# Values of the selected tokens by their own product in the last batch, and a new order of steps for the last two batches

## The chip, the core and the metric

The kernel runs on one core of a Trainium2 chip. The metric is the time of one execution on the device in microseconds (us), the median of several. The core has five engines that run side by side, each with its own queue of instructions in a fixed order: TensorE (PE in the profile: matmuls and transposes), VectorE (DVE), ScalarE (ACT), GpSimd (POOL) and SyncE (SP). SP, ACT and POOL also issue DMAs.

## What is computed

Two layers on x of 8 batches x 512 channels x 32 x 32 tokens, all in float32. Layer 0 is a group norm, attention with 8 heads over 1024 tokens and a residual. Layer 1, which the change is about, selects 256 of the 1024 tokens of each batch by the sum of their squares, lets these attend to each other, and puts the result in place of their values:

```
q, kk, v = wq x, wk x, wv x                      # over the channels
importance = sum(x * x over the channels);  idx = top 256
q_sel, k_sel = layer_norm(q[idx]), layer_norm(k[idx])
attn = softmax(clip(q_sel k_sel^T * 512**-0.5, -80, 80))
v[idx] = attn v[idx]
out = x + wo v
```

## The kernel before

Layer 0 takes most of the time; its values, x1, go to DRAM. Before layer 1 the matrices wv and wo are multiplied into one (`w["vo"]`), so that V of a token holds its contribution to the output, and the last product of the reference falls away: attended values are written over the rows of V, and V is only transposed and added to x1.

Layer 1 is written as small steps, each a function of a batch b and a number i (L235 to L547). For one batch they are, in order of the data:

- row (four transposes of x1 to rows of tokens), square (sum of squares on ScalarE), keep (copy of the rows to one of four buffers xT), put (a DMA from there to DRAM, sx)
- finite, spread, imp: the importances as a column and as a row; count (eight of them, VectorE): how many tokens are ahead of each; place, pick, holder, who: the indices of the selected tokens
- getx: GpSimd gathers the selected rows from sx. vo (four matmuls of 512 columns, in float32 eight records each), vkeep (copy to V in SBUF), vput (to DRAM, sv): V of 128 tokens; eight of these for a batch. getv gathers V of the selected tokens from sv to the tile vs
- selt, selk: the selected rows transposed to selT; qk (four products); stats, root, norm: layer norm; normt, scale: transposed and scaled; score, clip, exp, inv, probt, probk: softmax; att (two products with vs), attk, attput: result to DRAM, sa
- fetch (eight): GpSimd gathers from sa into V those rows that belong to selected tokens; back (eight): transposes of V; add (eight): plus x1, whose piece y was loaded by residual, and the store to the output. SP issues y's loads and the stores

The order on TensorE, VectorE, ScalarE and GpSimd is written out by hand as lists of words. BATCH holds one turn of the loop over the batches; a sign behind a word says how many batches ahead (+) or behind (-) the step works, so the work of several batches is interleaved. END is the list behind the last turn; in it a word without sign is of batch 7, one minus is batch 6, two are batch 5, and so on. Each engine executes its own steps of the list in that order and waits where data or a buffer isn't ready. SP's order isn't fixed by the list. All products and transposes of layer 1 write into PSUM tiles of one kind, of which there are eight in turn (bank, L221), so each waits for the readers of the tile eight before it. y has six buffers, and four loads are issued ahead (L520, L570).

Of the kernel before, what the change touches and what calls it, by code (L numbers as in the profile page):

```python
# [55 lines left out]

BATCH = """
# [13 lines left out]
vput7-- put2- keep1- add3---- square1- att0--- put1- holder-- inv--- who-- row0- vkeep6--  # L71
back4---- square2- row6- attk0--- row3- back7---- add7---- att1--- square0- back6----
add4---- row7- keep0- put4- square6- row5- keep6- keep7- attk1--- vo1- vo0- vput0-- put0-
getx-- square3- square5- add6---- keep3- attput--- square7- fetch1--- keep5- finite- selt1--
spread0- spread1- vkeep1- imp1- vput5-- imp0- put6- selt0-- fetch6--- count5- fetch5---
selk0-- fetch3--- selk1-- vo3- qk0-- count7- vkeep0- count6- count3- qk1-- fetch0--- put5-
qk2-- stats1-- stats0-- root1-- fetch2--- vkeep3- back0--- root0-- vo4- qk3-- stats2--
count2- fetch4--- root2-- norm0-- vput0- norm1-- vkeep4- put3- add0--- stats3-- root3--
normt0-- vo2- vput2-- norm2-- vput4-- vput6-- normt1-- row4 scale1-- norm3-- normt2--
normt3-- vput1-- vkeep2- scale2-- scale0-- square4 keep4 fetch7--- scale3-- count1- vo5-  # L80
count0- score1-- back5--- score0-- put7- add5--- clip-- vput3-- vo6- count4- place- vo7-
vkeep5- exp-- pick0- vkeep7- back3--- row1 probt-- vkeep6- back1--- inv-- add1--- probk--
row2 keep1 square2 square1 back2--- getv-- put1 back4--- att0-- add3--- add2--- vput1- keep2
row7 pick1- row0 row3 row6 put4 holder- keep0 square7 square3 back7--- put2 keep7 attk0--
add4--- who- add7--- att1-- row5 getx- square5 vo0 keep3 square0 attk1-- attput-- fetch5--
fetch4-- square6 put0 vput5- vo1 back6--- fetch1-- finite keep6 selt1- selt0- keep5 spread0
vkeep0 spread1 imp0 imp1 selk0- add6--- selk1- vo3 vput7- vput3- count2 vkeep1 fetch2--
# [29 lines left out]
def attention_then_topk_attention(  # L117
# [231 lines left out]
    def gather(name, pool, src):  # L349
        def step(b, _):  # L350
            t = get(pool, (name, b), [P, RT, C], name, 2)
            for rb in range(RT):
# [5 lines left out]
                    bounds_check=N - 1, oob_is_err=False,  # L358
                )
        return step  # L360


    def selt(b, j):
        pt = bank(("st", b, j)).rearrange("p (a n) -> p a n", n=TOP)
# [186 lines left out]
    def layer1():  # L551
        with ExitStack() as st:
# [16 lines left out]
            with tc.manual_schedule(engines=ORDERED):  # L569
                for _ in range(4):  # L570
                    residual(*next(loads))
# [646 lines left out]
```

## Time and profile before

| | us |
|---|---|
| median of 3 runs (2642.01 to 2644.24) | 2642.17 |
| the profiled execution | 2641.74 |
| its span, first to last instruction | 2640.0 |
| TensorE busy in it | 2578.1 (98%) |
| VectorE busy | 1922.1 (73%) |
| ScalarE busy | 1352.7 (51%) |
| GpSimd busy | 1163.8 (44%) |
| END, about | 2452 to 2640 |

Layer 1 begins at about 2120, layer 0 fills what is before. The profile's page cuts the span into 40 slices and gives each engine's busy share in tenths; the table of stretches has the busy us of PE, its weight loads, DVE, ACT and POOL in turn, then the granted clock of TensorE, the share of the DMA engines and GB/s. In lists of waits and in the timeline, "<-" names what ended an engine's idle time. In a timeline's line the numbers are the start, the time taken, the engine, the line of the kernel, the operation and its tiles, written to the left of "<-" and read to the right.

### The profile page before, as it was taken

The numbers are of one execution on the slowest core, as the hardware profiler recorded it, in microseconds if no ns is written. First come the engines' busy times: TensorE is split into PE (matmuls) and PEld (weight loads), VectorE is DVE, ScalarE is ACT, GpSimd is POOL, SyncE is SP. The second block draws the span as 40 slices with busy tenths as digits, with TensorE's granted clock in tenths as the row PEclk, the third lists the DMA queues.
The fourth block names the chain that finished last, engine by engine and source line by source line (L and its number), as shares of the span: only waits on it lengthen the run. The fifth ranks groups of instructions, "written<-read, shape, count | busy, mean of one in ns | idle before, by whom it ended". The sixth has DMA issues, their size and how long they took to land.

```text
span 2640.0 us, 27385 instructions
## 1 busy us (share of the span) xinstructions
PE 2578.1 (98%) x9916; PEld 1185.7 (45%) x9916; DVE 1922.1 (73%) x2434; ACT 1352.7 (51%) x1698; POOL 1163.8 (44%) x559
## 2 busy tenths in 40 slices
PE   7999999999999999999999999999999999999995
PEld 4444444444444444444444444444443345555553
DVE  5688868886878678867877787777767556666664
ACT  3556655565566456644665465556555433333331
POOL 0456645555455455544564465446545511211122
PEclk9999999999999999999999999999999999999998
DMA  3000001000100010011000100010002243555556
GB/s 132 1 5 32 1 24 56 17 1 31 58 9 1 32 64 1 1 32 64 0 1 32 64 1 7 27 64 1 13 28 88 76 168 124 199 203 203 196 187 199
DMA packets 79590, 161.21 MB, mean 61 GB/s; under 512 B 12106, under 2 KB 12106, under 8 KB 79456
## 3 DMA queue, kind: packets, MB, share of 16 engines
q1 hardware_dynamic: 52480, 113.27, 12.3%
q10 hardware_dynamic: 19296, 33.58, 3.4%
q0 software_dynamic: 7680, 12.61, 1.6%
q8 instruction: 79, 1.29, 0.2%
q14 instruction: 55, 0.45, 0.1%
HBM read 100.68 MB, written 71.30 MB: 65 GB/s over the span
## 4 chain that ended last, share of the span: by engine, by line
PE 90%; DMA 3%; DVE 3%; ACT 1%; issue 1%; POOL 1%; ACTq 0%; SPq 0%; POOLq 0%; DVEq 0%
PE sc L930 18%; PE av L989 17%; PE g L727 16%; PE g L748 8%; PE g L766 8%; PE b_pv L299 5%; PE b_pp L382 4%; PE ns L967 2%; PE den L1002 2%; PE pt L953 2%; DMA sx<-xT 1%; PE b_sc L448 1%; PE first L727 1%; PE b_po L527 1%; DMA y<-x1d 1%
## 5 line engine op out<-in xcount | busy, mean ns | idle before, releaser
L981 POOL TENSOR_TENSOR es<-es,e 128x1024 f32<-128x1024 f32 x384 | 913.6, 2379 | 345.2 <-ACT e L976 324.4
L938 ACT COPY e<-sc 128x1024 f32<-128x1024 f32 x512 | 508.1, 1013 | 568.4 <-PE sc L930 308.6
L973 DVE TENSOR_TENSOR e<-e,ns 128x1024 f32<-128x1024 f32 x512 | 603.9, 1206 | 2.5 <-PE ns L967 2.2
L976 ACT ACTIVATE e<-e 128x1024 f32<-128x1024 f32 x512 | 531.4, 1056 | 114.5 <-DVE e L973 107.8
L944 DVE TENSOR_TENSOR high<-sc,high 128x1024 f32<-128x1024 f32 x384 | 469.6, 1223 | 122.8 <-PE sc L930 56.8
L930 PE MATMUL sc<-q,k 64*128 64x512 f32 x2048 | 509.6, 615 | 4.8 <-DVE high L944 1.8
L989 PE MATMUL av<-e,v 128*64 128x512 f32 x2048 | 492.7, 602 | 0.0
L981 POOL TENSOR_TENSOR es<-e,e 128x1024 f32<-128x1024 f32 x64 | 151.4, 2366 | 706.6 <-ACT e L976 706.6
L727 PE MATMUL g<-x,wqkv 128*128 128x512 f32 x992 | 453.0, 599 | 0.0
L930 PEld LDWEIGHTS sc<-q,k 64*128 64x128 f32 x2048 | 176.0, 186 | 328.9 <-issue 180.6
L727 PEld LDWEIGHTS g<-x,wqkv 128*128 128x128 f32 x992 | 178.5, 190 | 228.0 <-issue 224.2
L989 PEld LDWEIGHTS av<-e,v 128*64 128x64 f32 x2048 | 129.9, 136 | 300.8 <-issue 293.7
L1014 DVE RECIPROCAL ri<-ri 128x512 f32<-128x512 f32 x64 | 214.6, 3353 | 26.2 <-ACT ri L1010 25.8
L748 PE MATMUL g<-wqkv,x 128*128 128x256 f32 x992 | 230.5, 385 | 0.0
L766 PE MATMUL g<-o,wp 128*128 128x512 f32 x472 | 219.9, 609 | 2.7 <-ACT V L313 2.7
L748 PEld LDWEIGHTS g<-wqkv,x 128*128 128x128 f32 x992 | 183.4, 190 | 68.0 <-issue 44.7
L299 PE MATMUL b_pv<-w,x 128*128 128x512 f32 x448 | 199.0, 592 | 0.0
L958 DVE TENSOR_REDUCE nm<-pt 128x8 f32<-128x1024 f32 x64 | 78.4, 1225 | 146.7 <-PE pt L953 146.4
L773 DVE SCALAR_TENSOR_TENSOR xr<-g,pb,xr 128x512 f32<-128x512 f32 x56 | 42.0, 749 | 170.8 <-PE g L766 170.8
L766 PEld LDWEIGHTS g<-o,wp 128*128 128x128 f32 x472 | 85.4, 191 | 134.1 <-issue 112.7
L1010 ACT COPY ri<-den 128x512 f32<-128x512 f32 x64 | 37.5, 585 | 178.6 <-PE den L1002 135.1
L299 PEld LDWEIGHTS b_pv<-w,x 128*128 128x128 f32 x448 | 82.5, 190 | 90.5 <-issue 90.2
(165 smaller groups left out, 1980.1 us busy)
## 6 DMA issues: line engine op xcount, KB each, us to landing
x<-in_x_dram SPq DMA_DIRECT2D x32, 512.0 KB
x<-x1d SPq DMA_DIRECT2D x32, 512.0 KB
sv<-V ACTq DMA_DIRECT2D x64, 256.0 KB
sx<-xT ACTq DMA_DIRECT2D x64, 256.0 KB
y<-x1d SPq DMA_DIRECT2D x64, 256.0 KB
out_dram<-y SPq DMA_DIRECT2D x64, 256.0 KB
xr<-in_x_dram SPq DMA_DIRECT2D x58, 256.0 KB
x1d<-xr SPq DMA_DIRECT2D x58, 256.0 KB
```

The costliest lines, as they stand in the source:

```text
L299: nc.tensor.matmul(pv, x1[b][:, k, ts(j, P)], w["vo"][:, k, :], start=(k == 0), stop=(k == CT - 1),)
L727: nc.tensor.matmul(pq, wqkv[:, k, ts(ot, P)], hs[b][:, k, ts(hf, HALF)], start=(k == 0), stop=(k == CT - 1),)
L748: nc.tensor.matmul(pv[:, ts(j, 2 * P)], hs[b][:, k, ts(2 * part + j, P)], wqkv[:, k, 2 * C + hm * 2 * P : 2 * C + (hm + 1) * 2 * P], start ...
L766: nc.tensor.matmul(po, wp[:, k, ts(mt, P)], os[b * NPAIR + k][:, ts(hf, HALF)], start=(k == 0), stop=(k == CT - 1),)
L930: nc.tensor.matmul(sc[:, hh, :], ks[p][r, ts(j, P)], qs[p][r, ts(hf, HALF)], start=True, stop=True,)
L938: nc.scalar.copy(raw[t, j], banks["s", t, j])
L944: nc.vector.tensor_tensor(high[t], banks["s", t, j], raw[t, 0] if j == 1 else high[t], ALU.max)
L973: nc.vector.tensor_tensor(raw[t, j], raw[t, j], high[t], ALU.add)
L976: nc.scalar.activation(raw[t, j], raw[t, j], AF.Exp, scale=QK_SCALE)
L981: nc.gpsimd.tensor_add(sums[t], raw[t, 0] if j == 1 else sums[t], raw[t, j])
L989: nc.tensor.matmul(avs[t][HD * hh : HD * hh + HD, :], vs[p // 2][:, j, (p % 2) * P + HD * hh : (p % 2) * P + HD * hh + HD], e[:, hh, :], s ...
L1014: nc.vector.reciprocal(dens[t], dens[t])
```

## The change

A new step vsel multiplies selT (the selected rows of x1, transposed, which qk uses anyway) by `w["vo"]`: four matmuls for each of two blocks of 128 selected tokens. vselk copies the result to the tile vs. In batch 7 alone these two take the place of getv, and the eight vput of batch 7 are left out, since nothing reads them. The vo steps of batch 7 stand among and behind the steps of its attention. The list END is new as a whole, also for batches 3 to 6; the other steps in it are the same ones, each as often as before. y gets eight buffers instead of six, and six loads are issued ahead instead of four.

```diff
--- before.py
+++ after.py
@@ -68,37 +69,36 @@
 getv- add2-- pick1 row2+ probt- vkeep7 row1+ probk- keep2+
 """
 END = """
-vput7-- put2- keep1- add3---- square1- att0--- put1- holder-- inv--- who-- row0- vkeep6--
-back4---- square2- row6- attk0--- row3- back7---- add7---- att1--- square0- back6----
-add4---- row7- keep0- put4- square6- row5- keep6- keep7- attk1--- vo1- vo0- vput0-- put0-
-getx-- square3- square5- add6---- keep3- attput--- square7- fetch1--- keep5- finite- selt1--
-spread0- spread1- vkeep1- imp1- vput5-- imp0- put6- selt0-- fetch6--- count5- fetch5---
-selk0-- fetch3--- selk1-- vo3- qk0-- count7- vkeep0- count6- count3- qk1-- fetch0--- put5-
-qk2-- stats1-- stats0-- root1-- fetch2--- vkeep3- back0--- root0-- vo4- qk3-- stats2--
-count2- fetch4--- root2-- norm0-- vput0- norm1-- vkeep4- put3- add0--- stats3-- root3--
-normt0-- vo2- vput2-- norm2-- vput4-- vput6-- normt1-- row4 scale1-- norm3-- normt2--
-normt3-- vput1-- vkeep2- scale2-- scale0-- square4 keep4 fetch7--- scale3-- count1- vo5-
-count0- score1-- back5--- score0-- put7- add5--- clip-- vput3-- vo6- count4- place- vo7-
-vkeep5- exp-- pick0- vkeep7- back3--- row1 probt-- vkeep6- back1--- inv-- add1--- probk--
-row2 keep1 square2 square1 back2--- getv-- put1 back4--- att0-- add3--- add2--- vput1- keep2
-row7 pick1- row0 row3 row6 put4 holder- keep0 square7 square3 back7--- put2 keep7 attk0--
-add4--- who- add7--- att1-- row5 getx- square5 vo0 keep3 square0 attk1-- attput-- fetch5--
-fetch4-- square6 put0 vput5- vo1 back6--- fetch1-- finite keep6 selt1- selt0- keep5 spread0
-vkeep0 spread1 imp0 imp1 selk0- add6--- selk1- vo3 vput7- vput3- count2 vkeep1 fetch2--
-count5 fetch0-- fetch3-- fetch7-- put5 count3 qk0- stats0- qk1- root0- count7 qk2- stats1-
-norm0- count6 root1- qk3- put3 vkeep3 stats2- stats3- vo2 vo4 put6 root2- root3- back0--
-norm3- norm2- norm1- fetch6-- vkeep2 count0 add0-- normt2- back5-- vput4- vput6- vkeep4
-normt1- normt3- scale2- vput4 normt0- add5-- scale3- scale1- vo5 scale0- score1- put7 vput2-
-count1 count4 place back1-- pick1 score0- back2-- vo6 vkeep5 clip- add2-- pick0 vo7 holder
-exp- probt- add1-- vput0 vkeep6 getv- vkeep7 probk- back3-- back4-- who back6-- att1- att0-
-inv- back7-- attk0- attk1- vput2 getx add3-- selt0 add4-- attput- selk0 add7-- fetch0-
-fetch7- selt1 selk1 vput6 fetch3- qk0 stats0 add6-- qk2 fetch1- qk1 root0 fetch2- stats2
-root2 norm2 stats1 root1 qk3 fetch6- norm0 back0- stats3 vput7 norm1 normt1 root3 vput3 norm3
-fetch4- vput1 normt2 fetch5- scale2 vput5 back1- normt3 scale3 normt0 scale1 scale0 add0-
-add1- getv score0 score1 clip back4- back5- back3- exp back6- probt probk att0 inv att1 attk0
-attk1 add4- attput add6- back7- fetch2 fetch3 fetch0 add5- fetch1 fetch4 back2 fetch6 add3-
-add2 back2- back6 fetch7 back4 fetch5 add2- add6 add7- back0 back3 add0 add4 add3 back5 add5
-back1 back7 add7 add1
+vput2-- put4- vkeep6-- row3- add3---- square2- holder-- att1--- back4---- row0- who-- inv---
+put2- row7- square1- keep1- attk1--- att0--- getx-- square3- keep3- keep0- keep7- put1- put3-
+put7- row5- back6---- attk0--- row6- square7- back7---- square6- add4---- square0- square5-
+keep5- keep6- put0- vput5-- vo1- put5- selt1-- finite- vkeep1- spread1- add6---- add7----
+selk1-- selt0-- spread0- imp1- imp0- attput--- count1- vo0- row6 row2 vput7-- selk0-- count6-
+keep6 keep2 row1 square2 count0- count2- vput6-- count7- row0 count3- vkeep0- square1 keep1
+put1 vput1-- qk0-- row7 qk1-- put6- square0 put2 stats1-- qk3-- stats0-- count5- put6 keep7
+square6 vo7- put7 root1-- vput1- fetch5--- row4 root0-- norm0-- qk2-- keep0 stats3--
+fetch3--- count4- vo6- place- square4 vkeep7- keep4 norm1-- square7 root3-- stats2-- row3
+vput0- vkeep6- vo4- normt1-- root2-- norm3-- normt0-- vput0-- row5 keep3 fetch1--- vput4--
+vput3-- norm2-- vkeep4- scale1-- normt2-- put3 normt3-- scale0-- fetch2--- pick1- scale2--
+square5 square3 keep5 put5 vo2- fetch0--- pick0- holder- finite spread0 scale3-- put4 vkeep2-
+imp0 getv-- fetch6--- spread1 who- imp1 score0-- back2--- count4 score1-- fetch7--- count2
+clip-- exp-- count3 vput2- back0--- count7 getx- vput4- count6 put0 add0--- vo3- count0
+fetch4--- probt-- vkeep3- probk-- inv-- add2--- att0-- att1-- attk1-- attk0-- selt1- selt0-
+selk1- selk0- attput-- count5 fetch6-- count1 qk3- place stats3- pick0 back3--- back4---
+vput6- add4--- root3- pick1 back1--- qk2- fetch4-- qk0- fetch0-- norm3- add3--- fetch2--
+vput7- back7--- stats2- stats0- holder fetch3-- fetch1-- qk1- who vput3- add7--- root0-
+root2- add1--- back5--- norm2- getx add5--- back6--- vo5- normt3- stats1- norm0- fetch7--
+root1- fetch5-- norm1- normt2- vkeep5- add6--- normt0- normt1- back2-- scale0- scale3-
+scale2- back5-- back7-- vput5- add2-- back1-- add1-- selt1 back6-- back3-- scale1- add7--
+add5-- score0- add6-- back0-- selt0 score1- selk1 add3-- clip- selk0 qk2 exp- stats2 back4--
+qk1 probt- probk- stats1 getv- add0-- qk0 qk3 att1- root2 root1 norm2 norm1 stats0 inv-
+stats3 add4-- root0 attk1- vo1 att0- root3 norm3 vkeep1 norm0 attk0- normt3 normt2 normt0
+attput- scale3 normt1 fetch5- scale0 scale1 fetch7- fetch6- vo0 vkeep0 scale2 score1 fetch1-
+score0 clip vsel1 fetch4- vo3 exp vselk1 vsel0 vselk0 probt fetch0- probk fetch2- vkeep3 vo6
+att1 inv fetch3- att0 vo7 vkeep6 vo2 back0- attk1 back2- back4- attk0 vkeep7 back3- attput
+vkeep2 add3- add0- back5- vo4 fetch7 fetch3 vo5 vkeep4 add2- back1- back7- fetch2 back6-
+fetch0 fetch1 add4- add1- fetch6 add7- add5- back2 back4 add4 add6- back0 back6 fetch4 vkeep5
+add0 fetch5 back3 back7 add2 back1 add6 back5 add3 add7 add1 add5
 """
 
 
@@ -359,6 +359,19 @@
                 )
         return step
 
+    def vsel(b, rb):
+
+        pv = bank(("sv", b, rb))
+        for k in range(CT):
+            nc.tensor.matmul(
+                pv, tiles["selT", b][:, k, ts(rb, P)], w["vo"][:, k, :],
+                start=(k == 0), stop=(k == CT - 1),
+            )
+
+    def vselk(b, rb):
+        t = get("mp", ("vs", b), [P, RT, C], "vs", 2)
+        nc.scalar.copy(t[:, rb, :], tiles["sv", b, rb])
+
 
     def selt(b, j):
         pt = bank(("st", b, j)).rearrange("p (a n) -> p a n", n=TOP)
@@ -517,7 +530,7 @@
 
     def residual(b, i):
         ct, hf = divmod(i, NH)
-        t = get("op", ("y", b, i), [P, HALF], "y", 6)
+        t = get("op", ("y", b, i), [P, HALF], "y", 8)
         nc.sync.dma_start(t, x1_dram[b][:, ct, ts(hf, HALF)])
 
     def back(b, i):
@@ -540,7 +553,7 @@
         "spread": spread_row, "imp": imp, "count": count, "vo": vo, "vkeep": vkeep,
         "vput": vput, "place": place, "pick": pick, "holder": holder, "who": who,
         "getx": gather("sel", "mp", x_dram), "getv": gather("vs", "mp", v_dram),
-        "selt": selt, "selk": selk, "qk": qk, "stats": stats, "root": root,
+        "vsel": vsel, "vselk": vselk, "selt": selt, "selk": selk, "qk": qk, "stats": stats, "root": root,
         "norm": normal, "normt": normt, "scale": scale, "score": score, "clip": clip,
         "exp": exp, "inv": inv, "probt": probt, "probk": probk, "att": att,
         "attk": attk, "attput": attput, "fetch": fetch, "back": back, "add": add,
@@ -567,7 +580,7 @@
 
             loads = iter([(b, i) for name, b, i in steps if name == "add"])
             with tc.manual_schedule(engines=ORDERED):
-                for _ in range(4):
+                for _ in range(6):
                     residual(*next(loads))
                 for name, b, i in steps:
                     if name == "load":
```

## The prediction

> **What bounds the kernel now.** I read the slices of the page first, then busy time by stretch, then TensorE's waits, then the last 35 us instruction by instruction.
>
> ```profile
> PE   7999999999999999999999999999999999999995
> ```
> ```profile
> 66.00:2100.00 2034.00, 2023.75 (x7809) 879.64 (x7808) 1566.29 (x1423) 1148.28 (x1269) 1045.23 (x446) 1.00 0.08 27
> ...
> 2540.00:2560.00 20.00, 20.00 (x69) 10.89 (x68) 17.41 (x57) 5.63 (x12) 1.01 (x2) 1.00 0.38 135
> ...
> 2580.00:2600.00 20.00, 15.97 (x52) 8.67 (x52) 13.85 (x43) 2.90 (x9) 10.00 (x10) 0.91 0.60 193
> 2600.00:2620.00 20.00, 10.03 (x48) 6.75 (x46) 6.97 (x12) 2.91 (x6) 2.83 (x3) 0.91 0.51 170
> 2620.00:2640.00 20.00, 6.06 (x36) 5.62 (x36) 6.73 (x10) 0.00 (x0) 5.18 (x6) 0.67 0.70 236
> ```
>
> The first column after the length is TensorE's busy time: full until 2580, then 32 of 60 us. So all that a new list for the last two batches can win lies in those 60 us; before them there is only something to lose. TensorE's waits from 2100 on, and the timeline of the end:
>
> ```profile
> PE b_po L527 <- DMA V<-sa,at: 12.3, 2, 10.7
> PE b_nt L421 <- DVE rows L411: 3.4, 2, 2.3
> ```
> ```profile
> 2608.50 3.70 PE L493 MATMUL b_pa<-vs,sT 128*128 128x512 f32 x8 [0.73 <-ACT sT L485]
> ...
> 2616.56 1.00 POOL L511 DMA_INDIRECT V<-sa,at  x1 [17.53 <-DMA sa<-att]
> ...
> 2623.29 4.20 PE L527 MATMUL b_po<-ident,V 128*128 128x128 f32 x21 [10.65 <-DMA V<-sa,at]
> ...
> 2629.13 1.86 PE L527 MATMUL b_po<-ident,V 128*128 128x128 f32 x15 [1.63 <-DMA V<-sa,at]
> ...
> 2636.26 0.69 DVE L535 TENSOR_TENSOR y<-b_po,y 128x512 f32<-128x512 f32 x1 [0.51 <-DMA out_dram<-y]
> ```
>
> The end is a serial chain of batch 7 (scores, softmax, att, sa written, eight gathers into V 1.3 us apart, transposes, add, store), with nothing left for TensorE beside it. From the end of att (2612.2) to the span's end it takes 27.8 us. Two more places show what the new list runs into, ScalarE at the start of END and the pace of one count on VectorE:
>
> ```profile
> 2460.48 0.59 ACT L246 COPY xT<-b_pt 128x512 f32<-128x512 f32 x1 [2.75 <-DMA sx<-xT]
> 2462.83 0.58 ACT L246 COPY xT<-b_pt 128x512 f32<-128x512 f32 x1 [1.77 <-DMA sx<-xT]
> ```
> ```profile
> 2470.65 0.88 DVE L281 TENSOR_SCALAR_CACHE_REDUCE junk<-imp,col 128x640 f32<-128x640 f32 x1 [3.40 <-ACT imp L269]
> ...
> 2472.50 1.15 DVE L281 TENSOR_SCALAR_CACHE_REDUCE junk<-imp,col 128x896 f32<-128x896 f32 x1
> ```
>
> A keep waits until the put that used its xT buffer (four of them) has landed: keep7 until 2462.8 for a put issued at 2452.65, 10 us, because the load of x1 of batch 7 (2 MB, issued from 2450.66) goes at the same time; later puts land in about 4.5 us. A count takes 2472.50 - 2470.65 = 1.85 us.
>
> **What the Trainium skill says.** "DMA: Bandwidth & Descriptors", Issuing engines are not separate DMA queues: transfers issued by different engines share the same 16 DMA engines and interleave. The trace agrees: ACT's puts are slow while SP's load runs. The same page, Anatomy of one DMA, gives about 2.0 us plus bytes over 436 GB/s, so 2.6 us for a store of 256 KB; the last store here takes 2637.0 to 2640.0, 3.0 us, which I use. "ScalarE: Activation LUTs", What ACT_TABLE_LOAD costs: 1283 ns for each load; the trace has 1283 ns. Both lists alternate root and exp batch by batch, so the number of loads stays.
>
> **The change part by part.** I count TensorE in issue time from 2452.2, when END's first att starts: eight records of vo or qk 3.44 us (16 take 6.87 in the chain), score 1.73, att 1.72, a group of four transposes 0.437 (8 take 0.87), holder 0.54. "P" is the sum of this work ahead of a step. END before sums to 154.0 us, so TensorE would end at 2606.2; it ends at 2631.0, so 24.8 us are waiting, nearly all behind 2577, where the trace is only 0.9 us behind P.
>
> *Added:* two vsel, 2 x 3.44 = 6.9 us on TensorE (P total 160.9), and two vselk, 2 x 0.59 on ScalarE, which has 5.8 us of work in the last 60. *Removed:* eight vput and getv of batch 7, 2.5 MB. getv went at 2596.73 and was not waited for, so its removal saves nothing by itself; what counts is that att no longer needs vo of all tokens, so vo can be moved.
>
> *Moved, batch 7.* att0 ended at P 149.6 and ends at P 140.1 now; vo 1, 0, 3, 6 (13.8 us) fill the chain ahead of it and vo 7, 2, 4, 5 stand behind it. In the tail of the new list I find every link covered: scores end at P 122.5, clip takes 4 x 0.69 = 2.75 us, exp 1.4, so probt could go at P 127 and stands at 132.8 behind vsel1, vo3, vsel0. The 2.3 us wait of normt on rows goes too: vo1 and att0 stand ahead of normt.
>
> *Moved, rows of batch 7* from P 41-66 to 16-44, batch 6's squares as a block behind keep0 and keep7 on ScalarE. Here is the first loss. Batch 6's spread1 stands at P 11.4 (2463.6), spread0 at 12.2; they were at P 15.7. Ahead of them ScalarE must do keep0 (waits for put4, issued at about 2452) and keep7 (put2), then four squares at 0.8, finite, keep5. With landings of 8 to 10 us keep0 goes at 2460-2462, the squares end at 2466.0-2467.2, and selt1, whose PSUM bank is freed by square0, and spread0, whose bank is freed by keep5, go at 2468-2469 in place of 2464.4. Loss 3.3 to 4.3, I take 4.0. Were the puts to land in 5 us, it would be about 1.
>
> *Moved, counts of batch 7* from P 79-108 to 52-63, into the same stretch as norm of batch 6. Second loss. From imp1 of batch 7 (needs spread1, ends P 50.3, plus 1.1 us for the copies: P 51.4) VectorE has, before norm1 of batch 6 is done: 8 counts x 1.85 = 14.8; clip 2.75; 7 adds x 0.65 = 4.5; 2 attk 1.45; inv 0.2; place 0.6; 4 stats x 1.03 = 4.1; 2 pick 2.3; 4 norm x 1.70 = 6.8; who 0.35: 37.8 us, so P 89.2. normt0 of batch 6 wants it at P 84.5. Loss 4.7; less if the copies go sooner, 4.5 taken. It is not on top of smaller stalls inside the stretch (probt and att of batch 5 with no other matmul between them, some 2 us; qk3 behind selk, some 2 us): those are paid out of the same 4.5. Before, the norms of batch 6 had 24 us of VectorE work in 24 us of P, and the 2540:2560 row has VectorE at 17.4 of 20: already close.
>
> *Queues passed.* POOL: getv of batch 5 now stands ahead of fetch6, 7, 4 of batch 4 and getx of batch 6, and waits for vput3 of batch 5, issued at about P 45. It then goes at about 2503, and four gathers (5.2 us) behind it put getx of batch 6 at 2509-2512; landing takes 3.4, so 2515; selt1 wants it at P 61.9 + 4 = 2518. Three us to spare, cost nothing; if vput3 lands 5 us later, 2 us. The fetches of batch 4 have 10 us to spare. SP: attput of batches 4 to 7 stand among stores and loads as before. ACT: sixteen puts and eleven vputs in the first 53 us in place of eight and nine; counted under the rival on puts.
>
> *y from 6 to 8 buffers, 6 ahead.* VectorE waited 4.2 us for y loads, all in the last 5 us; elsewhere nothing. More buffers can help only there. Cost elsewhere nothing.
>
> *Tail, from the end of att0 at P 140.1.* attk 1.0, attput, landing 3.54 (2613.02 to 2616.56): 144.7. Eight gathers x 1.3 would end at 155, but fetch5 needs vkeep5, and vo5 ends at P 156.1, so it goes at 157.0 and lands 3.4 later (2625.70 to 2629.13): 160.4. Four groups of transposes: 162.2. On VectorE batch 6's adds begin at 149 and go at 0.65, the last one could be at 164. The loads of the last four y wait for the stores of items eight earlier, and these adds are at 157-159: store lands at +3.0, SP issues stores and loads at 0.65 each, so the last load goes at 164 and lands in 4 to 5.4 us (2630.89 to 2636.26): add at 169, store 3.0 to 3.7: P 172.5. So 32.4 us from att's end against 27.8 before: part of the win is given back, since four vo and all adds of two batches now fall together there. Bounds: 29 if the loads land in 3 us, 36 if 7 MB in 23 us (317 GB/s; peaks in END are 400) hold each other up.
>
> **Sum.** att0 ends at 2452.2 + 140.1 + 4.0 + 4.5 = 2600.8 instead of 2612.2: 11.4 won; 4.6 given back in the tail: span 2633.2. The profiled execution took 2641.74 for a span of 2640.0, so 1.7 more: 2634.9. The median is 0.4 above that execution: 2635.3, taken as 2635, 7 us (0.27%) faster.
>
> **Rivals.** *A, the waits I price do not come* (puts land in 5 us, VectorE overlaps better): 8.5 less 1 to 2 us: 2627-2628. For it: before, 125 us of END went with 0.9 us of waiting, in the same resources. Against: the 10 us landing is in the trace, and the sum on VectorE has little to give. Chance 0.20. *C, much the same*: the tail takes its upper bound (+3.6) and the stretches of batches 5 and 6 stall apart and not in one (+3): 2641. Chance 0.21. *B, slower*: the xT buffers. Sixteen puts go through four buffers between 2457 and 2498, three rounds of 13.6 us; some 3 us go between a keep and its put's issue, so landings up to 10 us fit. At 15 us each round is 5 late, squares and all of ScalarE stand behind the waiting keep, finite of batch 7 comes 15 us later, and with it imp1 and VectorE's 37.8 us: 2650. It decides above a mean landing of about 13 us. For it: 10.2 us was seen once; against: 4.5 us when the x1 load is over. Chance 0.17. That the change doesn't do what it says I exclude: V of the selected rows is x_sel times the same joint weight. My forecast: 0.42, own range 2630 to 2640.
>
> **How the numbers follow.** What can be told from no change is about 0.2%, 5.3 us: faster is below 2636.9, slower above 2647.5. Faster: 0.20 from A, 0.37 of mine, 0.01 of C: 0.58. Same: 0.05 of mine, 0.19 of C: 0.24. Slower: 0.17 from B, 0.01 of C: 0.18. The range 2627 to 2651 leaves out about half of B and a third of A.
>
> **What would show it.** Right: TensorE near full until about 2600 except for 4 us about 2465 (waiting for squares and keeps) and 4 to 5 us in 2510-2545 (waiting for VectorE's norm, clip, exp); att of batch 7 ending near 2601; no 10 us wait on V; last adds waiting for y loads. Wrong: att of batch 7 ending after 2608, keeps waiting over 10 us each, or a tail over 36 us.

## The result, and the profile after

| | kernel before | changed kernel |
|---|---|---|
| median, us (22 runs each, one chip) | 2642.21 | 2638.32 |
| lowest to highest | 2639.61 to 2647.19 | 2636.6 to 2642.19 |
| ratio, 95% interval | | 0.9985 [0.9978, 0.9991] |
| the profiled execution, its span | 2641.74, 2640.0 | 2641.48, 2639.8 |

The change saves 3.9 us. The prediction said 2635.0, 7 us saved, with a range of 2627 to 2651; the measured gain is a little over half of that. By the prediction's own bound (faster is below 2636.9) the time is "much the same", to which it gave a chance of 0.24. The range is 24 us wide and holds the time of the kernel before too, so that it held says little. The profiled execution of the changed kernel is 3.2 us above its median, so its span hardly differs from that of the kernel before. The changed kernel was therefore run once more, unaltered. There it took 2638.67, with 2643.66 for the kernel before on that chip (ratio 0.9979 [0.997, 0.9987]), and that profiled execution, of 2638.0 us from first to last instruction, is used below beside the first.

The page's slices and the busy time by stretch (length, then PE, weight loads, DVE, ACT, POOL, clock, share of the DMA engines, GB/s) of the changed kernel, first execution:

```profile
PE   7999999999999999999999999999999999999998
```
```profile
2460.00:2470.00 10.00, 6.13 (x29) 3.53 (x27) 1.35 (x2) 2.79 (x7) 0.00 (x0) 1.00 1.03 398
2470.00:2480.00 10.00, 8.28 (x26) 5.25 (x27) 6.27 (x18) 4.74 (x11) 5.00 (x5) 0.66 0.86 289
...
2580.00:2600.00 20.00, 20.00 (x71) 11.45 (x70) 5.39 (x10) 5.94 (x13) 7.97 (x8) 1.00 0.17 53
2600.00:2620.00 20.00, 20.00 (x63) 10.05 (x62) 3.98 (x6) 3.33 (x7) 5.98 (x6) 1.00 0.25 83
2620.00:2640.00 20.00, 7.63 (x51) 5.67 (x49) 7.63 (x12) 0.59 (x1) 1.99 (x2) 0.78 0.83 286
```

Between 2580 and 2620 TensorE is now busy all 40 us (26 before). But a hole has come at 2460 to 2480 that wasn't there, with a lower clock behind it, and the last 20 us are hardly fuller than they were (7.6 us busy, 6.1 before). In the kernel before, the stretch in which the hole begins was

```profile
2460.00:2470.00 10.00, 9.73 (x35) 5.10 (x34) 0.34 (x2) 5.05 (x13) 0.00 (x0) 1.00 1.05 407
```

The DMA engines were as full there (407 GB/s), and ScalarE waited twice for a put, but nothing that TensorE wanted at once stood behind these waits. So what is new is not that the DMA engines are full, but what stands behind the waiting steps. TensorE's waits in the last 200 us of the first execution:

```profile
PE b_pi L263 <- ACT xT L246: 5.6, 1, 5.6
PE b_po L540 <- DMA V<-sa,at: 1.6, 1, 1.6
PE b_pa L506 <- ACT sT L498: 0.9, 1, 0.9
PE b_pp L395 <- ACT selT L386: 0.7, 1, 0.7
PE b_nt L434 <- DVE rows L424: 0.5, 1, 0.5
```

The wait of 10.7 us for V is gone and spread1 (L263) waits 5.6 us in its place. Since an execution can enter the list END up to 2.8 us later or 1.6 us earlier than the one shown of the kernel before (see the last section), the rest is read from one step: the first transposes of V (b_po) after 2430, which stand at the same point of every list here. The numbers are us behind that step; only the tail counts from the end of att0.

| execution | spread1 | next rows | first back behind norm | att0 of batch 7 ends | tail from there to the end |
|---|---|---|---|---|---|
| before | | | | 179.9 | 27.8 |
| changed, first | 36.6 | 44.3 | 115.9 | 171.6 | 33.1 |
| changed, second | 36.6 | 42.9 | 114.8 | 170.1 | 34.0 |

So att0 of batch 7 came 8 to 10 us earlier, and 5 to 6 us of that went back in the tail. (Spread1 is batch 6's, rows batch 7's. "First back behind norm" is the first transpose of V behind the norms of batch 6.)

### The profile page after: what moved, and what is told of

Read it like the earlier page. It is cut to its first block, busy times and chain, and to the rows that moved or that the text cites. A ratio compares the mean times of both kernels' runs of the same rounds, so it can differ in the third digit from the quotient of the medians.

```text
span 2639.8 us, 27404 instructions
## 1 busy us (share of the span) xinstructions
PE 2586.0 (98%) x9932; PEld 1190.0 (45%) x9932; DVE 1920.2 (73%) x2434; ACT 1354.1 (51%) x1700; POOL 1161.1 (44%) x557
## 5 line engine op out<-in xcount | busy, mean ns | idle before, releaser
L524 POOL DMA_INDIRECT V<-sa,at x64 | 64.0, 1001 | 149.4 <-DMA sa<-att 54.6
```

## The experiments

The ratio is always to the kernel before on the same chip; the changed kernel's are 0.9985 and 0.9979. The expectations call keep0, keep7 and spread1 at the start of END steps of batch 7 or of the last stage; by the list they carry one minus, so they are of batch 6.

### The changed kernel once more

> The changed kernel once more, unaltered, for a second profiled execution. The profile shown of it was of an execution some 3 us above its median, entered the last list 2.2 us later than the kernel before did, and is the only one of five executions of lists of this kind in which the step who of batch 7 (VectorE) did not sit idle for about 2 us. Theory 1: the late entry was of that execution alone: this one enters the last list within 1 us of the kernel before; keep0 of batch 7 waits 5.5 to 6.5 us for its put and spread1 over 5 us as before. Theory 2 (the wait at who comes where VectorE arrives early there, and so takes back part of any time saved ahead of it): here who waits 1 to 3 us too, and the profiled time is within 2 us of the median 2638. Rival: entry 2 us late again (then the change costs time at the change of layers), and no wait at who.

Measured: 2638.67, 13 runs. Entry 1.6 us behind the kernel before (2433.94 against 2432.34), where the first execution had 2.8. Both waits are there again, on TensorE and on ScalarE:

```profile
2464.22 0.60 PE L380 MATMUL b_st<-ident,sel 128*128 128x128 f32 x4
2470.52 1.08 PE L263 MATMUL b_pi<-ident,col 128*128 128x128 f32 x4 [5.70 <-ACT xT L246]
...
2473.11 3.90 PE L299 MATMUL b_pv<-w,x 128*128 128x512 f32 x8
```
```profile
2453.62 0.39 ACTq L249 DMA_DIRECT2D sx<-xT  x1
...
2463.02 0.59 ACT L246 COPY xT<-b_pt 128x512 f32<-128x512 f32 x1 [5.47 <-DMA sx<-xT]
2464.97 0.59 ACT L246 COPY xT<-b_pt 128x512 f32<-128x512 f32 x1 [1.36 <-DMA sx<-xT]
2465.04 2.03 ACTq L249 DMA_DIRECT2D sx<-xT  x3
2467.12 0.60 ACT L243 ACTIVATE sq<-b_pt 128x512 f32<-128x512 f32 x1 [1.57 <-issue]
```

put4 is issued at 2453.62; keep0, which needs its buffer, goes at 2463.02, 9.4 us later. Then keep7, three puts, and only then the first of four squares that spread1 needs. There was no wait at who, so theory 2 fell for this execution; whether it holds for every one of this kernel is taken up below, at the load. Theory 1 put the entry within 1 us of the kernel before and the rival at 2 or more; 1.6 lies between them.

### Six xT buffers

```diff
-        nc.scalar.copy(get("r1", ("xT", b, j), [P, C], "xT", XT), tiles["pt", b, j])
+        nc.scalar.copy(get("op" if b else "r1", ("xT", b, j), [P, C], "xT",
+                           XT + 2 if b else XT), tiles["pt", b, j])
```

> The changed kernel, but the rotated tiles (xT) of batches 1 to 7 have six buffers of their own in place of the four shared ones; nothing else is moved. Theory 1 (the four xT buffers: keep0 and keep7 of batch 7 wait for the landing of put4 and put2, hold the squares behind them and with them spread1): keep0 no longer waits about 6 us, spread1 of the last stage starts within 1 us of selt1, TensorE's clock in the 20 us behind it stays above 0.9 where it was 0.66, and the batch of the last stage is 6 to 9 us earlier by its square-root tile; time 2629 to 2633 us, some 6 to 9 below the changed kernel's 2638.3. Rival 1 (the squares are late by ScalarE's own sum of work, whatever the buffers do): time within 2 us of 2638. Rival 2 (a time saved here is lost again at the counts of batch 7, because VectorE's sum sets the later stall): spread1 is early, yet the time falls by under 3 us.

Measured: 2638.52, ratio 0.9979 [0.9972, 0.9987]. From the entry on, spread1 comes at 33.6 and the rows at 40.0, 3 us sooner; the first back stands at 114.9 and att0 ends at 170.7, both as in the changed kernel. Rival 2 came true in its timing: the time saved is gone again before the norms are done. Its reason, VectorE's own sum of work, is not what the trace shows. ScalarE and VectorE:

```profile
2453.79 1.57 ACT L246 COPY xT<-b_pt 128x512 f32<-128x512 f32 x3
2457.58 3.34 ACTq L252 DMA_DIRECT2D sx<-xT  x3
2460.97 0.60 ACT L243 ACTIVATE sq<-b_pt 128x512 f32<-128x512 f32 x1 [5.61 <-DMA x<-x1d]
```
```profile
2533.47 0.15 DVE L408 TENSOR_SCALAR ve<-mv 128x1 f32<-128x1 f32 x1
2535.82 0.16 DVE L349 TENSOR_REDUCE who<-b_pn 128x2 f32<-128x4 f32 x1 [2.19 <-remote]
```

The keeps no longer wait. But the three puts behind them now sit at their issue, and the squares stand behind the puts. The profile, which infers what ended a wait, names the landing of the load of batch 7 (x<-x1d); by the program a put needs only its keep, so why it stands there is open. And on VectorE the step who idles 2.2 us, with the norms of batch 6 behind it.

### Squares ahead of keep0 and keep7

```diff
-... keep1- attk1--- ... keep3- keep0- keep7- put1- put3- put7- ... square7- square6- square0- square5-
+... keep1- put1- ... keep3- put3- square0- square7- ... square5- square6- keep0- keep7- put7-
```

> The changed kernel, four xT buffers as before; only the order of ten steps near the start of the last list is another: put1 stands right behind keep1, put3 right behind keep3, and the squares of chunks 0, 7, 5 and 6 stand ahead of keep0 and keep7, which still wait for a landing. Theory 1 (the wait of keep0 alone costs nothing, only what stands behind it in ScalarE's order): spread1 starts 3 to 6 us sooner, the clock stays above 0.9, time 2631 to 2635 us. Rival (the landing itself is on the path, since the transposes of chunks 5 and 6 and the tiles behind them still wait for keep0 and keep7, so that the stall only moves a few steps on): time 2636 to 2639 us.

Measured: 2637.14, ratio 0.9977 [0.9968, 0.9985]. Spread1 at 33.1, rows at 39.6, att0 at 172.0. The timing is the rival's, the way is another: put3 itself waited 5.55 us at its issue, by the profile for an earlier put, with the squares behind it, and who waited 2.3 us later on. (The profiled execution, of 2641.23, was the slowest of the 12.) Through who the gather of batch 7 starts late, and selt behind it.

### The load behind the puts, and counts without ties

Both have one run. The first moves the emission of the load, the second leaves out a part of the counts of batch 7, as its expectation says.

```diff
+            steps.remove(("load", B - 1, 0))
+            steps.insert(steps.index(("put", B - 2, 7)) + 1, ("load", B - 1, 0))
```

> The changed kernel, with the 2 MB load of batch 7 of layer 1 (or the load of the last item) issued after the eight puts of batch 6 and not ahead of them. Theory 1b (the puts land late because they share the DMA engines with that load): put4 lands in under 6 us where it took 10, keep0 waits under 2 us, spread1 is 3 to 6 us earlier. Rival (the put takes its 10 us by itself, at its queue or its own transfer): keep0 waits 6 us as before. In both the last batch's own rows may now wait for their load, so the whole time is not what this run is read by.

The edit did nothing to the load: SP's order isn't fixed by the list, and SyncE issued it at 2450.64, ahead of put4 as before. keep0 waited 6.02 us. The question stayed open until the last run.

The run, of 2643.28, still tells something, since TensorE, VectorE, ScalarE and GpSimd have the same orders as in the changed kernel. Here who waited 2.58 us, and the step behind it came later:

```profile
2547.47 0.33 PE L434 MATMUL b_nt<-ident,rows 128*128 128x128 f32 x1 [1.48 <-issue]
2549.15 1.11 PE L434 MATMUL b_nt<-ident,rows 128*128 128x128 f32 x4 [1.36 <-DVE rows L424]
2550.70 3.62 PE L540 MATMUL b_po<-ident,V 128*128 128x128 f32 x16
```

TensorE waited 2.8 us around the normalised rows (0.8 in the second execution of the changed kernel), and the sixteen transposes behind took 3.62 us instead of 1.91, at a clock of 0.75 between 2550 and 2560. From the next rows to the end of att0 it took 132.6 us; both executions of the changed kernel took 127.2. So in this execution the wait at who came with nothing saved ahead of it, and 5.4 us more were gone before att0. In one execution the two came together; that the wait makes the loss isn't shown. In the runs with six buffers and with the squares the same stretch took 130.7 and 132.4 us.

```diff
+        if b == B - 1:
+            if j == 4:
+                nc.vector.memset(cnt[:, 2, :], 0.0)
+            return
         nc.vector.scalar_tensor_tensor(
```

> The changed kernel, with a part of the computation left out in the last batch of layer 1: the counts of equal entries (ties), which are set to zero there; the eight steps of counts give VectorE about 3.4 us less. Theory (the second loss is a row of short waits for results just made, and VectorE's sum is only one of them): att0 of batch 7 ends 0 to 1.5 us earlier. Rival (VectorE's sum over the 37 us between imp1 of batch 7 and norm1 of batch 6 is the bound of that stretch): the stalls between there and the batch-6 multiply vanish, and att0 of batch 7 ends 2.5 to 3.4 us earlier.

Measured: 2640.8. att0 ended at 171.6, 1.5 us later than in the second execution of the changed kernel and no earlier than in the first, so not even the small gain came. VectorE had idle time in the stretch, 1.9 us of it at who again. The run excludes nothing about VectorE's sum, because the wait at who came in its place. Beside the run of the load, which had that wait too, it is 3.9 us shorter from the next rows to att0 (128.7 against 132.6), which speaks for VectorE's sum as a part of the bound; with one execution of each it shows nothing.

### Fewer fetches ahead of who

In the four runs with six buffers, squares, load and counts, who began 8.51 or 8.52 us after the first of six fetches that GpSimd issues in a row for batch 5 (2527.31 and 2535.82 with six buffers). So the next run took three of the six out of the row.

```diff
-... fetch6-- ... fetch4-- qk0- fetch0-- ... fetch2-- ... holder fetch3-- fetch1-- qk1- who ... getx ...
+... fetch6-- ... fetch4-- qk0- fetch0-- ... holder qk1- who ... getx fetch2-- fetch3-- fetch1-- ...
```

> The first experiment (six xT buffers of their own), and on top of it three of the six fetches of batch 5 that GpSimd issues in a row ahead of the gather of batch 7 (chunks 2, 3 and 1) moved behind that gather; nothing else is moved. In four executions the step who of batch 7 on VectorE sat idle 1.9 to 2.6 us and began 8.5 us after the first of the six fetches, which is 0.9 to 1.0 us after the sixth. Theory (that row of fetches holds who, and behind who on VectorE the norms of batch 6): who does not wait, norm1 of batch 6 ends about 2 us sooner against the first experiment, TensorE's two waits of 1.4 us at the transposes of the normalised rows shrink to under 0.7 us together, and the time falls 1.5 to 3 us below the first experiment's, to a ratio of 0.997 or less. Rival (who waits for the holder product itself, whatever GpSimd does): who waits 2 us as before, and the ratio stays at 0.998.

Measured: 2640.3, ratio 0.9989 [0.9981, 0.9996], a worse ratio than with six buffers alone. The first half of the theory holds: who doesn't wait,

```profile
2534.34 0.15 DVE L407 TENSOR_SCALAR ve<-mv 128x1 f32<-128x1 f32 x1
2534.41 0.15 DVE L348 TENSOR_REDUCE who<-b_pn 128x2 f32<-128x4 f32 x1
```

and the first back could go at 111.7, 3 us sooner. But the rows it transposes are now fetched last:

```profile
PE b_po L542 <- DMA V<-sa,at: 5.3, 3, 3.6
```

TensorE waits 3.6 us for them ahead of att0, which ends at 173.9; the other two of the three waits are in the tail. The fetches were not idle work that can stand anywhere.

### All of it together

```diff
-... keep0- keep7- put1- put3- put7- row5- ... square5- keep5- keep6- put0- ...
+... keep0- keep7- row5- ... square5- keep5- keep6- put1- put3- put7- put0- ...
-... fetch6-- ... fetch4-- ... fetch0-- ... fetch2-- ... fetch3-- fetch1-- ... getx ... fetch7-- ... fetch5-- ...
+... fetch2-- fetch5-- fetch7-- ... getx fetch1-- fetch6-- fetch3-- fetch0-- fetch4-- ...
```

> The changed kernel with six xT buffers of their own, with put1, put3 and put7 of batch 6 behind the squares (in the first experiment put3 or put7 waited at its issue until the 2 MB load had landed, with the squares behind it), and with the row of six fetches of batch 5 cut to three (chunks 2, 5 and 7, which are transposed first; the other five behind the gather of batch 7, in the order in which they are transposed, so that the wait of 3.6 us for a late fetch of the run e8_fetch goes). Theory (the first loss is keep and put ahead of the squares; what was saved there was taken back at who, whose wait is the row of fetches; with both gone it stays saved): spread1 waits under 1 us, the clock stays above 0.95, who does not wait, no wait for V over 1 us before 2600; att0 of batch 7 ends 6 to 9 us earlier against the entry of the last list than in the changed kernel (there 152.2 us after), time 2629 to 2633 us, ratio 0.995 to 0.9965. Rival (VectorE's or TensorE's chains take it back again, at norm or at the scores of batch 7): att0 earlier by under 3 us, ratio over 0.997.

Measured: 2643.47, ratio 0.9997 [0.9988, 1.0005]: nothing of the gain of the change is left. Spread1 goes at 30.7 and the rows at 35.5, without any wait: 7.4 us sooner than in the changed kernel. Then ScalarE stands still, and TensorE with it:

```profile
2464.36 2.30 ACTq L251 DMA_DIRECT2D sx<-xT  x4
2471.70 0.33 ACTq L318 DMA_DIRECT2D sv<-V  x1
...
2473.11 0.58 ACT L315 COPY V<-b_pv 128x512 f32<-128x512 f32 x1 [8.17 <-DMA V<-sa,at]
```
```profile
2460.00:2470.00 10.00, 9.78 (x43) 5.61 (x41) 1.57 (x4) 3.18 (x8) 1.39 (x2) 1.00 1.05 405
2470.00:2480.00 10.00, 6.25 (x14) 3.50 (x15) 4.67 (x14) 5.64 (x13) 3.59 (x4) 0.66 0.77 249
```

The DMA engines carry 405 GB/s until 2470, as in the changed kernel (398), with a mean share of 0.96 already from 2454 to 2460, and the hole in TensorE's time has moved from 2460-2470 to 2470-2480 with the lower clock behind it. Of the 8.17 us ahead of vkeep1 the four puts took 2.30 at their issue; then ScalarE stood at vput until 2471.70 and at vkeep1. After that TensorE waited 4.1 us for V ahead of att0, the price of the fetches' new order, and att0 ended at 177.0.

### The product alone

The kernel before with only the new product, and then with two tiles of V moved behind attention as well:

```diff
-... vput4 ... vput0 ... vput2 ... vput6 ... vput7 ... vput3 ... vput1 ... vput5 ... getv score0 score1 clip ...
+... norm1 vsel1 vselk1 normt1 ... score0 score1 clip vsel0 vselk0 ...
```
```diff
-... vo6 ... vo7 ... vkeep6 ... vkeep7 ... attk1 add4- attput ...
+... attk1 add4- vo6 vo7 vkeep6 vkeep7 attput ...
```

> The kernel before with its own last list, in which only the product takes the gather's place: the eight vput and the getv of batch 7 are gone, vsel1 and vselk1 stand ahead of normt1, vsel0 and vselk0 behind clip; all else, the y buffers too, is as before. Theory (the product alone brings nothing as long as the list still makes all eight tiles vo of batch 7 ahead of attention; the gain of the change is in the list that moves two of them behind it): ratio 0.9985 to 1.0015. Rival (the puts and the gather held the end up, and the product alone brings the gain): ratio 0.998 to 0.9985, as in the changed kernel.

> The kernel before with the product in place of the gather, as in the run h1_product, and besides with vo6 and vo7 of batch 7 and their copies moved from the middle of its list to right ahead of attput of batch 7, behind the last product of attention. Six tiles vo are still made ahead of attention, where the changed kernel leaves two ahead of the last scores. Theory (what the change wins is TensorE work moved behind attention, into the time in which the attention rows are stored and fetched; the product by itself costs): 6.9 us of TensorE work leaves the path ahead of att0, part of which the waits there eat; ratio 0.9975 to 0.9995, at least 4 us below h1_product. Rival (the other new orders of the list matter, not the tiles moved): within 2 us of h1_product, ratio 1.0005 to 1.0018.

Measured: 2646.73, ratio 1.0012 [1.0005, 1.0018], and 2644.36, ratio 1.0004 [0.9995, 1.0013]. The product by itself costs 3 us: att0 ends 5.9 us later than before (185.7), since vsel1 and vsel0 (3.44 us each) stand in the serial chain. Moving two tiles (6.9 us of TensorE) wins 1.3 us at att0 (184.5); in the old list that room fills with waits, TensorE waited 3.25 us for VectorE's pick. The second lies between its theory and its rival. So the product with two moved tiles makes no gain in the old list. That the rest of the new list makes it is argued: the changed kernel leaves four tiles behind att, and no run separates them from the order of the other steps. In the new list the next rows, with which the chain of batch 7 begins, stand 43 us behind the entry; in the old list they stand at 62. In both runs the vputs of batch 7 are left out, as in the change; the two more buffers of y, with two more loads ahead, have no run of their own.

### The tail

```diff
-... vselk0 probt ... vo6 ... att0 vo7 vkeep6 vo2 back0- attk1 back2- back4- attk0 vkeep7 back3- attput ...
+... vselk0 back3- back5- add3- add5- probt ... back1- back7- add1- add7- vo6 ... att0
+back0- add0- back2- add2- back4- add4- back6- add6- vo7 vkeep6 vo2 attk1 attk0 vkeep7 attput ...
```

> The changed kernel, with the sixteen back and add steps of batch 6 moved up: four of them behind vselk0 of batch 7, four ahead of vo6 and eight ahead of vo7, instead of behind the last product of attention. They are the same steps; TensorE's work ahead of the last product grows by eight groups of four transposes (0.44 us each, 3.5 us), and the tail behind attput loses them. Theory 3 (the tail of 33 us is set by the last adds of batch 7, which wait for their y loads, which wait for the stores of batch 6, so late adds of batch 6 cost time): att0 of batch 7 ends up to 3.5 us later, the last adds no longer wait for y loads, the tail falls to 24 to 27 us, time 2632 to 2635 us. Rival (the tail is the chain attput, fetch, transposes, add, store of batch 7 alone, which starts at att0): time 2638 to 2642 us, the tail shorter only by what att0 is later.

Measured: 2637.45, ratio 0.9974 [0.9964, 0.9983]; att0 at 172.0, tail 29.8. Only four groups of transposes (1.75 us), not eight, stand ahead of att0 in this list, the expectation miscounted. The last adds wait for no load any more, but attput went out at 2610.38 where it had been 2604.84, since the four adds ahead of attk held VectorE and their stores and loads held SyncE. The next run moves just these:

```diff
-back0- add0- back2- add2- back4- add4- back6- add6- vo7 vkeep6 vo2 attk1 attk0 vkeep7 attput
+back0- back2- back4- back6- vo7 vkeep6 vo2 attk1 attk0 vkeep7 attput add0- add2- add4- add6-
```

> The run e5_tail with one thing mended: the adds of chunks 0, 2, 4 and 6 of batch 6 stand behind attput of batch 7, not ahead of attk1 and attk0, where they held VectorE 2.5 us and, with their stores and loads ahead of it on SyncE, held the issue of attput 5.5 us beyond the changed kernel's. Theory (in e5_tail the last adds waited no longer for their y loads, but the late attput and the fetches behind it took most of that back): attput is issued 3 to 5 us sooner than in e5_tail (at 2605.5 to 2607.5 us where it was at 2610.4), the last add starts at 2626 to 2629, time 2632 to 2635 us, ratio 0.9955 to 0.997. Rival (the tail is bound by vkeep5 and the fetch behind it, which e5_tail did not move): time 2636 to 2638, ratio 0.997 to 0.998.

Measured: 2631.35, four runs from 2631.23 to 2633.41, ratio 0.9956 [0.994, 0.9973]. This is the changed kernel with the new tail alone. All four runs are below the fastest of its 35 (2636.6). att0 at 172.0, tail 26.0. SyncE and VectorE of the changed kernel (second execution), and then of this one:

```profile
2604.84 0.37 SPq L518 DMA_DIRECT2D sa<-att  x1
2613.39 2.12 SPq L549 DMA_DIRECT2D out_dram<-y  x4
2615.57 5.52 SPq L534 DMA_DIRECT2D y<-x1d  x4
...
2627.51 0.45 SPq L534 DMA_DIRECT2D y<-x1d  x1
...
2630.02 1.31 DVE L548 TENSOR_TENSOR y<-b_po,y 128x512 f32<-128x512 f32 x2 [4.72 <-DMA y<-x1d]
```
```profile
2598.92 2.48 SPq L533 DMA_DIRECT2D y<-x1d  x4
2604.35 0.37 SPq L517 DMA_DIRECT2D sa<-att  x1
2604.95 2.54 SPq L548 DMA_DIRECT2D out_dram<-y  x4
2607.91 2.57 SPq L533 DMA_DIRECT2D y<-x1d  x4
...
2623.67 2.48 DVE L547 TENSOR_TENSOR y<-b_po,y 128x512 f32<-128x512 f32 x4 [1.26 <-PE b_po L539]
```

In the changed kernel the last load of y is issued at 2627.5, and the last four adds wait for loads, the first of them 4.7 us. With batch 6 stored earlier, all loads are out by 2610.5, in a stretch in which the DMA engines of the changed kernel had a share of 0.25 to 0.35, and the last four adds follow the transposes. The tail is 7.1 to 8.0 us shorter. Some 1.7 us of that are TensorE's, whose last transposes end 21.4 us behind att0 instead of 23.1, since transposes of batch 6 left the tail too; the rest is the order of batch 6's stores and batch 7's loads of y, which was the tail's bound.

### The load from GpSimd

```diff
-            nc.sync.dma_start(t[:, c, :], x1_dram[b][:, c, :])
+            (nc.gpsimd if b == B - 1 else nc.sync).dma_start(t[:, c, :], x1_dram[b][:, c, :])
...
+            steps.remove(("load", B - 1, 0))
+            steps.insert(steps.index(("getx", B - 3, 0)) + 1, ("load", B - 1, 0))
```

> The kernel of the run e10_tail2, with the 2 MB load of batch 7 issued by GpSimd behind its gather of batch 5 (near 2459) and not by SyncE ahead of the last list (near 2453); four shared xT buffers as in the changed kernel. Theory 1b, which the run e6_load left open, since SyncE issued the load at its old time there (the puts of batch 6 land after 10 us because they share the DMA engines with that load): put4 lands in 5 to 7 us, keep0 waits 1 to 3 us where it waited 5.7 to 6.2, spread1 starts 3 to 5 us earlier against the entry of the last list, TensorE's clock stays above 0.9 there; the rows of batch 7 may wait up to 3 us for the load. Of that, who takes back about 2 us, so that the whole is 2628 to 2631 us, ratio 0.9945 to 0.9955. Rival (the DMA engines are full from 2454 to 2472 whatever the order, and the wait only moves to the load): put4 quicker, but spread1 or the rows of batch 7 late by as much, 2631 to 2634 us, ratio 0.9955 to 0.9965.

Measured: 2637.36, ratio 0.9975 [0.9965, 0.9984]; the rival, and worse than it said. The run has the new tail, so it is 5 us slower by its ratio than the run before.

```profile
2452.21 0.39 ACTq L248 DMA_DIRECT2D sx<-xT  x1
...
2457.11 1.23 ACT L245 COPY xT<-b_pt 128x512 f32<-128x512 f32 x2 [0.98 <-issue]
2457.83 1.84 ACTq L248 DMA_DIRECT2D sx<-xT  x3
...
2465.56 0.58 ACT L245 COPY xT<-b_pt 128x512 f32<-128x512 f32 x1 [2.99 <-DMA sx<-xT]
2469.21 0.58 ACT L245 COPY xT<-b_pt 128x512 f32<-128x512 f32 x1 [3.07 <-DMA sx<-xT]
```

put4 lands in under 4.9 us now (2452.21 to keep0 at 2457.11), so at least 4.5 of the 9.4 us were the load's doing, and spread1 goes at 30.7. But then keep5 and keep6 wait 3 us each for puts that share the engines with the later load, and the rows come at 43.7. Who waited 2.5 us here too, and att0 ended at 176.7.

## Why the prediction was right, point by point

The direction held, and so did the range, which had room for no change too. The size did not: in the profiled span the forecast gain of 6.8 us came out at 3.6 (second execution, without the difference at entry: 179.9 + 27.8 less 170.1 + 34.0). The time lies between the forecast (2635) and rival C (2641). Of the signs named beforehand, att of batch 7 ended at 2606.7 and 2604.0, between "right" (2601) and "wrong" (2608). The errors in single steps were larger than the error of the sum, and in part they cancelled.

*Where TensorE's time would go.* Right: full until 2600 but for a wait near 2465, no 10 us wait on V, the last adds waiting for their loads. The wait of 4 to 5 us for VectorE in 2510 to 2545 did not show as such (second loss).

*First loss, "Loss 3.3 to 4.3, I take 4.0".* The mechanism was right: keep0 and keep7 wait for landings, the squares stand behind them, spread1 behind those. The size was not. With no wait at all spread1 comes at 30.7 and the rows at 35.5 (all of it together); in the changed kernel they come at 36.6, and at 42.9 and 44.3. Of the 7.4 and 8.8 us lost, 5.9 are lost by spread1: the 4.0 of the prediction and the three puts between keep7 and the squares, which took 2.0 us at their issue, where a put alone takes 0.33 to 0.39. The rest, 1.5 and 2.9 us, goes between spread1 and the rows at a lower clock of TensorE: the four transposes take 1.06 to 1.09 us instead of 0.60, and the next vo, eight records, 3.90 and 5.29 us instead of 3.60. The prediction has no term for the clock, though three of the lines that it shows have 0.91, 0.91 and 0.67. The Trainium skill, "TensorE: Matmul & The Clock Gate", What's actually happening, says that the clock goes to half after an idle window of about 3.4 us and comes back after as long a busy one. The runs agree in kind: behind the wait of 5.6 us in the first execution the granted clock is 0.50 from 2472 to 2476 and 1.00 again from 2478. But it was 0.50 also behind shorter waits, of 2.7 us (six buffers, 2466 to 2468) and of 2.0 us (squares, 2468 to 2470). The two executions differ in when it fell. In the second it was 0.50 already from 2468 to 2470, still within the wait, and 1.00 again from 2474, so less of the low clock met work.

*Second loss, "4.7; less if the copies go sooner, 4.5 taken".* By TensorE's issue times the changed kernel loses 3.1 us between the rows and att0, in both executions. Its listed waits there are 0.9 us for ScalarE's sT, 0.7 for selT, and only 0.5 to 0.8 for VectorE's rows. So the two smaller stalls inside the stretch, which the prediction counted as paid for by the wait for VectorE, came, and the wait for VectorE was the smaller part. VectorE itself took about as long as forecast: from the first count of batch 7 to the last norm 36.3 us in the first execution (2513.84 to 2550.1), with no idle time over 0.3 us, where the sum said 37.8. That this sum bounds att0 is not shown: the run with lighter counts wasn't faster, because who waited.

*The two losses are not independent.* The prediction added them. Each run that took the first one away lost as much again before att0, at who, or at another landing. For the landing of put4 the cause is shown by the last run, which took the load out of its way. That the DMA engines are full from 2460 to 2470 (398 and 405 GB/s) holds for the kernel before as well (407); the order chooses which step waits, and what stands behind it.

*Tail, "32.4 us from att's end against 27.8 before".* 33.1 and 34.0. The working was right: the last loads wait for stores of batch 6. Moving batch 6's steps took 7 to 8 us out of the tail, most of it by these stores.

*"What counts is that att no longer needs vo of all tokens, so vo can be moved".* Only as part of a new list: the product alone was slower, and with two tiles moved it was no faster than before.

*Rivals.* B, landings of 15 us, did not come: put4 took 9.4 to 10.1 us, and ScalarE waited there only in the first round. A did not come either: the puts did not land in 5 us, and only the second loss was smaller than forecast. Of C, the tail took 0.7 to 1.6 of its 3.6 us, and att0 still ended 8 to 10 us earlier.

Added up for the second execution, the predicted span of 2633.2 becomes 2633.2 + 1.2 (END's first step on TensorE at about 2453.4, not 2452.2) + 3.4 (first loss 7.4 for 4.0) - 1.4 (second, 3.1 for 4.5) + 1.6 (tail) = 2638.0; measured 2638.0. The terms were measured in that execution, so this shows that none is left out, and not what made each.

## What to carry to other kernels

These are readings of the runs above, not rules. In a stretch where the DMA engines are full, ask which step waits for a landing and what stands behind it on its engine. More buffers (six xT), another order (squares, all of it together) and a later load (the last run) each passed the wait on to another step that issues or needs a transfer. In a tail, look first for stores that free the buffers of later loads: moving them into a stretch in which the DMA engines had little to do was worth most of 7 to 8 us here when they stood behind attput, on which the chain depends, and 3 to 4 us for the whole tail when they stood ahead of it. And a new operation that shortens a data path can be worth nothing until the list around it is changed: alone it cost 3 us.

## What was not expected of the hardware

*The wait at who.* By the program who waits for TensorE's holder product alone, which is done 2.2 to 3.7 us earlier (by 2532.25 in the run with six buffers). In five executions it still idled 1.9 to 2.6 us, began 8.50 to 8.52 us after the first of six fetches in a row on GpSimd and about 1 us after the sixth; in four others with the same six fetches (changed kernel twice, both tail runs) it didn't wait, though VectorE came to it at the same distance from the first fetch (5.9 to 6.2 us, against 5.9 to 6.6). The run of the load waited with the very orders of the changed kernel, which didn't. With three fetches ahead it didn't wait in two of two. What holds it is open.

*Entry.* The same instructions ahead of END end at 2430.8 to 2435.1 in different executions. In the first of the changed kernel TensorE's clock was 0.69 and 0.63 in the two stretches of 5 us from 2155 to 2165, at the change of layers; in the kernel before it was 1.00 there. The old list was entered at 2431.6 to 2432.5 in three executions, the new ones at 2430.8 to 2435.1 in eleven, so a small cost of the change ahead of END is neither shown nor excluded. A difference of 2 us in a span says little about a list unless it is read from a common step.

*A put at its issue.* An issue by ScalarE took 0.33 to 0.39 us alone; three in a row took 1.3 to 3.3 us. While one waited the whole engine stood, 5.6 us at puts and, in the run with all of it together, up to 8.2 us at four puts, a vput and the vkeep behind it. What ended these waits is inferred by the profile.
